# A two-layer attention, memory and expert network on one core: later turns, earlier fetches, and the memory's gradient on another engine

## The chip, the cores and the metric

The kernel runs on one core of a Trainium2 chip. The metric is the device time of one execution in microseconds (us). The engines are named as in the profile: PE is TensorE (matmuls), PEld its weight loads, DVE is VectorE, ACT is ScalarE, POOL is GpSimd, and SP is SyncE, which here issues nearly all DMA transfers from one in-order queue.

## The reference

The input `x` has 16 sequences of 512 tokens with 128 features, in float32. There are two layers, and each adds two branches to its input:

```python
xn = layernorm(x)
x  = x + memory(xn) + block0(xn)     # layer 0
xn = layernorm(x)
x  = x + attn1(xn) + moe1(xn)        # layer 1
```

`memory` is a small network that is trained while it reads. The sequences are cut into 8 chunks of 64 tokens, and the chunks follow one another; in each, the gradient of a loss is taken over all sequences at once:

```python
def mem_fwd((w0, w1, ln), x):
    h = silu(x @ w0.T); y = h @ w1.T
    return x + rmsnorm(y, ln)
loss  = mean((v_c - mem_fwd(p, k_c))**2 * th_c)
grads = grad(loss)(mem)
clip  = min(1 / (sqrt(sum(sum(g*g) for g in grads)) + 1e-6), 1)
surp  = eta_c * surp - grads * clip
mem   = beta_c * mem + surp
...
return mem_fwd(mem_f, q)             # read-out of all tokens with the final memory
```

`block0` is a convolution over tokens, attention with 16 heads of 8 features, a layernorm, and 8 experts of width 512 that all see every token and are weighted by a softmax gate. `attn1` is causal attention with 16 heads; its context goes through a convolution, and the result is used as the queries of a second causal attention over the same keys and values. `moe1` sends each token to 8 of 32 small experts.

## The kernel before

The kernel is written as Python generators, its stages. A loop, `Turns.run`, goes round all live stages in turns and lets each do one step per turn, up to its next `yield`. PE executes in the order in which the steps were written (`ORDERED`); the other engines' instructions are placed by a scheduler, which keeps those of the later stages of a turn behind the newest maximum (`issue_after`). So the number of turns, and what PE does in each, are fixed when the program is built. `idle(n)` lets n turns pass, `after(...)` waits until a named mark is set, with `lag=n` for n turns more, and `fill` puts in a matmul without use where a turn has too little work for PE.

**Attention.** The backbone of nearly every turn is one group of scores in each of two passes. `largest` computes scores (`s<-kx,qx`) into a PSUM buffer of which there is one (`p1=1`), and DVE takes their maxima `nm` (L387 for causal groups of 512 or 384 columns, which add the mask and reduce in one instruction; L396 otherwise). With causal attention the groups of 256 and 128 columns are packed two or four heads to a buffer; their diagonal blocks get the mask by an add, one for each of the two row groups `r` (L395), before L396. The maxima are transposed, go out to `top`, and come back as two more rows of the queries `qx` (L413 to L417). Some turns later, set by `lag` in `back`, `weighted` computes the scores the other way round (`s<-qx,kx`, also with one buffer), ACT takes the exponential `e`, POOL cuts it to the causal triangle (L471), and PE multiplies with the values (`pc`).

**Experts of layer 0.** `ffn(b)` handles one sequence: it loads the accumulator `ac` and the transposed tokens `x1T`, fetches the weights `ew1` and `ew2` of expert 0, idles 2 turns, and then runs 64 units, `first(i)` (hidden layer, `phe` and ACT's `hTe`) and `second(i)` (back to the features, `pye`). A credit of `TURN` ns per turn, less the other PE work of the turn, says how many units run. Each weight is fetched one expert ahead. `x1T` has one buffer, the weights two each.

**Memory.** `scan` runs the 8 chunks one after the other beside the attention of layer 0. `step(c)` turns the keys, computes the hidden layer (`hidden`), and then the gradient in two halves of four token tiles: `gradient(0)` from turn 7 of the step, `gradient(1)` from turn 11. With `yh` the normalised output and `kv` keys minus values, DVE computes `gq = yh*ln*ln + kv*ln` in one half's buffer; POOL had made `kv*ln` (L878) and `ln*ln` (L813). `m` is the row mean of `gq*yh`, and `gq + yh*m`, scaled by ACT, is the gradient that goes back. The gradient of the norm's weight `ln` is made apart from it: `norm_gradient`, from turn 16, lets POOL compute `gy = (yh*ln + kv)*yh*th` over all eight tiles in four passes of 128x1024 (L904 to L910). It first waits until the projections of chunk c+1 are read, since `gy` shares its buffer with their input `xc`. `project(c)` makes keys and values two chunks ahead.

**Read-outs.** After the last chunk, `readout(b)` starts every 6 turns: it projects the queries, normalises them (POOL, L1000 and L1001), idles 3 turns, transposes them, applies the memory, and copies the result to `yq`, always in the buffer `hT1`; POOL adds the rest and the sum is stored to `acc` (L1035).

**Layer 1.** From turn `t0` on, `middle(b)` starts every 44 turns; `front1(b)` loads the transposed tokens and, after 2 turns, projects them.

## Time and profile before

| | |
|---|---|
| runs, median (lowest to highest) | 3922.72 us (3920.65 to 3936.18), 3 runs |
| the profiled execution, its own time | 3921.06 us |
| its span in the profile | 3919.1 us |
| PE busy, of the span | 3463.3 us (88%) |
| DVE, ACT, POOL busy | 2389.2, 2152.6, 1658.1 us |
| mean granted TensorE clock | 0.960 |
| DMA moved | 370.50 MB, mean 95 GB/s |

The profile is of one execution. Its busy times are sums over the span; a row of the groups gives source line, engine, operation, what is written and read, the count, busy time, mean time of one, and the idle time just before with what ended it. Times inside the span, such as "at 335 us", count from its start. In this execution the last read-out is stored at 1581.5 us, and layer 1's attention fills most of the rest.

### The profile page before, as it was taken

The numbers are of one execution on the slowest core, as the hardware profiler recorded it, in microseconds if no ns is written. First come the engines' busy times: TensorE is split into PE (matmuls) and PEld (weight loads), VectorE is DVE, ScalarE is ACT, GpSimd is POOL, SyncE is SP. The second block draws the span as 40 slices with busy tenths as digits, with TensorE's granted clock in tenths as the row PEclk, the third lists the DMA queues.
The fourth block names the chain that finished last, engine by engine and source line by source line (L and its number), as shares of the span: only waits on it lengthen the run. The fifth ranks groups of instructions, "written<-read, shape, count | busy, mean of one in ns | idle before, by whom it ended". The sixth has DMA issues, their size and how long they took to land. (4 is left out here: it accounts for less than half of the span.)

```text
span 3919.1 us, 62028 instructions
## 1 busy us (share of the span) xinstructions
PE 3463.3 (88%) x22267; PEld 1898.2 (48%) x22267; DVE 2389.2 (61%) x5187; ACT 2152.6 (55%) x3687; POOL 1658.1 (42%) x2562
## 2 busy tenths in 40 slices
PE   5889888889899888999999999999999999987877
PEld 2445444445444444445555555555555555543343
DVE  5666646665665545546466666666666666667762
ACT  1555655665566666555555555555555555543443
POOL 5433542453342544323344344424443344333674
PEclk7999999999999999999999999999999999998998
DMA  5222212221322332433434433443334333433343
GB/s 159 64 64 70 67 51 80 64 67 39 106 69 87 95 86 77 128 87 104 123 94 117 113 112 102 110 122 111 104 107 121 107 113 101 120 97 84 83 91 86
DMA packets 289938, 370.50 MB, mean 95 GB/s; under 512 B 46008, under 2 KB 141408, under 8 KB 289248
## 3 DMA queue, kind: packets, MB, share of 16 engines
q1 hardware_dynamic: 282464, 359.73, 32.1%
q0 software_dynamic: 7168, 6.82, 1.1%
q8 instruction: 176, 2.88, 0.3%
q14 instruction: 130, 1.06, 0.1%
HBM read 236.59 MB, written 133.25 MB: 94 GB/s over the span
## 5 line engine op out<-in xcount | busy, mean ns | idle before, releaser
L467 ACT ACTIVATE e<-s 128x1024 f32<-128x1024 f32 (+1 forms) x1216 | 1190.7, 979 | 702.7 <-PE s L192 637.0
L396 DVE TENSOR_REDUCE nm<-s 128x2 f32<-128x1024 f32 (+1 forms) x704 | 861.2, 1223 | 683.9 <-PE s L192 676.3
L387 DVE CUSTOM_DVE_ANT_0 s<-s,sb_const 128x512 f32<-128x512 f32 (+1 forms) x1024 | 647.6, 632 | 543.1 <-PE s L192 524.3
L471 POOL TENSOR_SCALAR_AFFINE_SELECT e<-e 128x128 f32<-128x128 f32 (+2 forms) x1408 | 467.8, 369 | 1003.2 <-ACT e L467 1000.9
L192 PE MATMUL s<-kx,qx 64*128 64x512 f32 (+3 forms) x3072 | 622.0, 432 | 236.8 <-DVE nm L396 132.1
L192 PEld LDWEIGHTS s<-kx,qx 64*128 64x128 f32 x3072 | 275.2, 188 | 895.6 <-issue 275.3
L192 PE MATMUL pc<-e,vp 128*32 128x512 f32 (+3 forms) x6144 | 642.3, 506 | 26.9 <-POOL e L471 26.5
L585 PEld LDWEIGHTS pye<-ew,hTe 128*128 128x128 f32 x4096 | 514.7, 195 | 141.4 <-issue 126.0
L585 PE MATMUL pye<-ew,hTe 128*128 128x128 f32 x4096 | 581.7, 286 | 0.8 <-DMA ew<-in_ew 0.8
L577 ACT ACTIVATE hTe<-phe,sb_cols 128x512 f32<-128x512 f32 x512 | 353.7, 691 | 404.7 <-PE phe L192 402.8
L192 PE MATMUL phe<-x1T,ew 128*128 128x512 f32 x1024 | 538.4, 610 | 14.1 <-DMA x1T<-x1d 6.7
L192 PE MATMUL s<-qx,kx 64*128 64x512 f32 (+3 forms) x3072 | 511.3, 359 | 34.3 <-ACT e L467 25.7
L593 POOL TENSOR_TENSOR ac<-ac,y 128x512 f32<-128x512 f32 x128 | 164.8, 1288 | 399.7 <-ACT y L592 397.4
L192 PEld LDWEIGHTS s<-qx,kx 64*128 64x128 f32 x3072 | 290.3, 190 | 77.1 <-ACT e L467 54.6
L395 DVE TENSOR_TENSOR s<-s,sb_const 128x256 f32<-128x256 f32 (+1 forms) x384 | 199.9, 521 | 150.8 <-PE s L192 138.4
L192 PEld LDWEIGHTS pc<-e,vp 128*32 128x32 f32 x6144 | 151.9, 110 | 255.8 <-issue 172.9
L192 PEld LDWEIGHTS phe<-x1T,ew 128*128 128x128 f32 x1024 | 160.2, 196 | 32.4 <-issue 8.2
L592 ACT ACTIVATE y<-pye,pr 128x128 f32<-128x128 f32 x512 | 146.6, 369 | 42.7 <-PE pye L585 37.9
L387 DVE DVE_READ_ACCUMULATOR2_ANT nm<- 128x1 f32 x1024 | 144.7, 141 | 0.0
L199 PE MATMUL fill<-sb_pb,sb_const 128*128 128x512 f32 (+2 forms) x238 | 122.5, 603 | 10.8 <-DMA sb_pb<-in_pb 10.4
L205 POOL TENSOR_SCALAR rs_t<-ss 128x4 f32<-128x4 f32 (+1 forms) x56 | 12.0, 215 | 197.4 <-ACT sq L258 195.8
L967 POOL TENSOR_TENSOR cl<-cl,phalf 128x1 f32<-128x1 f32 x8 | 4.5, 568 | 190.1 <-ACT cl L966 190.1
(294 smaller groups left out, 3991.8 us busy)
## 6 DMA issues: line engine op xcount, KB each, us to landing
ew<-in_ew SPq DMA_DIRECT2D x256, 256.0 KB
kx<-rk SPq DMA_DIRECT2D x192, 256.0 KB
qx<-rq SPq DMA_DIRECT2D x128, 256.0 KB
rq<-hi SPq DMA_DIRECT2D x64, 256.0 KB
rq<-lo SPq DMA_DIRECT2D x64, 256.0 KB
rk<-hi SPq DMA_DIRECT2D x64, 256.0 KB
rk<-lo SPq DMA_DIRECT2D x64, 256.0 KB
qx<-r SPq DMA_DIRECT2D x64, 256.0 KB
```

The source lines that it names most:

```text
L192: nc.tensor.matmul(o, lhsT=lhsT, rhs=rhs, start=start, stop=stop)
L199: nc.tensor.matmul(o[:, 0:n], lhsT=ident, rhs=cell[0][:, 0:n], start=True, stop=True)
L205: nc.gpsimd.tensor_scalar(t, src, scale, eps, ALU.mult, ALU.add)
L387: newest[0] = nc.vector.tensor_tensor_reduce(out=sv[:, r, 0, :], in0=sv[:, r, 0, :], in1=row["caus"][:, S - n :], scale=1.0, scalar=-BIG, ...
L395: nc.vector.tensor_tensor(dg, dg, bc(row["caus"][:, S - P :], 1, per), ALU.add)
L396: newest[0] = nc.vector.tensor_reduce(nm[:, qt, :, t : t + per], sv, AX.X, ALU.max)
L467: nc.scalar.activation(e[:, :, 0 : per * n], s[:, :, 0 : per * n], AF.Exp, scale=SCALE)
L471: cleared[0] = nc.gpsimd.affine_select(out=ev[:, r, :, 0:P], in_=ev[:, r, :, 0:P], pattern=[[0, per], [1, P]], compare_op=ALU.is_ge, fill= ...
L577: nc.scalar.activation(hs[i], ph, AF.Relu, bias=col("fb", i))
L585: nc.tensor.matmul(pye[0][:, t, :], lhsT=h[:, t * P : (t + 1) * P], rhs=w2[e][:, f, :], start=(f == 0 and t == 0), stop=(f == 3), skip_gro ...
L592: nc.scalar.mul(y[:, t, :], pye[0][:, t, :], pr[:, t, e : e + 1])
L593: nc.gpsimd.tensor_tensor(ac, ac, y, ALU.add)
```

## The change

1. The causal mask is added to both row groups by one instruction instead of two.
2. `fetch0(b)` loads `x1T` and starts the fetches of expert 0. The last `first` unit of `ffn(b-1)` calls it, if the tokens are ready; otherwise `ffn(b)` does and idles 3 turns.
3. The gradient of the memory and that of the norm's weight are made from shared products: `gy = (yh*ln + kv)*yh` per half on DVE, then `gy*ln` for the row mean, and POOL only multiplies `gy` by `th`. `norm_gradient`, `ln2` and the product `kv*ln` are gone. The second half starts at turn 9, not 11.
4. A read-out idles 5 turns before its transpose, and keeps its result in the buffers of `h` and `ds` by turns.
5. `back` lags 5 turns behind the maxima, not 4; `front1` idles 3 turns, not 2.
6. `t0` is 480; it was the turn in which the scan ended, 482, where that is later.

```diff
-                    for r in range(2):
-                        dg = sv[:, r, :, n - P : n]
-                        nc.vector.tensor_tensor(dg, dg, bc(row["caus"][:, S - P :], 1, per), ALU.add)
+                    dg = sv[:, :, :, n - P : n]
+                    nc.vector.tensor_tensor(dg, dg, bc(bc(row["caus"][:, S - P :], 1, per), 1, 2), ALU.add)
...
+    def fetch1(w1, w2, e):
+        w1[e] = ff.tile([P, DFF], F32, tag="ew1", bufs=2, name="ew1")
+        nc.sync.dma_start(w1[e], a["ew1"][:, e, :])
+
+    def fetch2(w1, w2, e):
+        w2[e] = ff.tile([P, 4, D], F32, tag="ew2", bufs=2, name="ew2")
+        nc.sync.dma_start(w2[e], a["ew2"][:, e])
+
+    def fetch0(b):
+
+        x1T = ff.tile([P, S], F32, tag="x1T", bufs=1, name="x1T")
+        nc.sync.dma_start(x1T, x1d[1, b])
+        fetched[b] = x1T, {}, {}
+        fetch1(*fetched[b][1:], 0)
+        fetch2(*fetched[b][1:], 0)
...
-        x1T = ff.tile([P, S], F32, tag="x1T", bufs=1, name="x1T")
-        nc.sync.dma_start(x1T, x1d[1, b])
-        w1, w2 = {}, {}
...
-        fetch1(0)
-        fetch2(0)
-        yield from idle(2)
+        if b not in fetched:
+            fetch0(b)
+            yield from idle(3)
+        x1T, w1, w2 = fetched.pop(b)
...
             nc.scalar.activation(hs[i], ph, AF.Relu, bias=col("fb", i))
+            if i == n - 1 and ("x1", b + 1) in done:
+                fetch0(b + 1)
...
             def before():
-                nc.gpsimd.tensor_tensor(ln2, ln, ln, ALU.mult)
...
-                nc.gpsimd.tensor_tensor(tq, kv[:, a4, :], bc(ln, 1, 4), ALU.mult)
                 yield from idle(3)
                 nc.vector.tensor_tensor(yq, yq, bc(ry[:, a4], 2, D), ALU.mult)
                 nc.gpsimd.tensor_tensor(tr[:, a4], ry[:, a4], th[:, a4, c], ALU.mult)
                 yield
-                nc.vector.tensor_tensor(gq, yq, bc(ln2, 1, 4), ALU.mult)
-                yield
-                nc.vector.tensor_tensor(gq, gq, tq, ALU.add)
-                yield
-                nc.vector.tensor_tensor(tq, gq, yq, ALU.mult)
-                yield
+                nc.vector.tensor_tensor(gq, yq, bc(ln, 1, 4), ALU.mult)
+                yield
+                nc.vector.tensor_tensor(gq, gq, kv[:, a4, :], ALU.add)
+                yield from after(("read", c + 1) if c + 1 < NC else ("read", c))
+                if q == 0:
+                    late["gy"] = s1.tile([P, NT, D], F32, tag="gy", name="gy")
+                gy = late["gy"][:, a4, :]
+                yield
+                nc.vector.tensor_tensor(gy, gq, yq, ALU.mult)
+                yield
+                nc.vector.tensor_tensor(tq, gy, bc(ln, 1, 4), ALU.mult)
+                yield
+                nc.gpsimd.tensor_tensor(gy, gy, bc(th[:, a4, c], 2, D), ALU.mult)
                 nc.vector.tensor_reduce(m[:, a4], tq, AX.X, ALU.add)
                 nc.vector.tensor_scalar(m[:, a4], m[:, a4], -1.0 / D, None, ALU.mult)
                 yield
+                nc.vector.tensor_tensor(gq, gq, bc(ln, 1, 4), ALU.mult)
+                yield
                 nc.vector.tensor_tensor(tq, yq, bc(m[:, a4], 2, D), ALU.mult)
-                yield
                 nc.vector.tensor_tensor(gq, gq, tq, ALU.add)
+                yield
                 yield
                 for t in range(4):
                     nc.scalar.mul(gq[:, t, :], gq[:, t, :], tr[:, 4 * q + t : 4 * q + t + 1])
-                yield
-
-            def norm_gradient():
-
-                yield from after(("read", c + 1) if c + 1 < NC else ("read", c))
-                gy = late["gy"] = s1.tile([P, NT, D], F32, tag="gy", name="gy")
-                nc.gpsimd.tensor_tensor(gy, yh, bc(ln, 1, NT), ALU.mult)
-                yield
-                nc.gpsimd.tensor_tensor(gy, gy, kv, ALU.add)
-                yield
-                nc.gpsimd.tensor_tensor(gy, gy, yh, ALU.mult)
-                yield
-                nc.gpsimd.tensor_tensor(gy, gy, bc(th[:, :, c], 2, D), ALU.mult)
...
-                (7, gradient(0)), (11, gradient(1)), (16, norm_gradient()),
+                (7, gradient(0)), (9, gradient(1)),
...
             nc.gpsimd.tensor_tensor(q, q, bc(rq, 2, D), ALU.mult)
-            yield from idle(3)
+            yield from idle(5)
...
-            y = s1.tile([P, TB, D], F32, tag="hT1", name="yq")
+            y = s1.tile([P, TB, D], F32, tag=("h", "ds")[b % 2], name="yq")
...
-        yield from after(("tops", layer, b, i, c), lag=4)
+        yield from after(("tops", layer, b, i, c), lag=5)
...
         nc.sync.dma_start(xT, xt[1, b])
-        yield from idle(2)
+        yield from idle(3)
...
-    TBB, t0 = 44, max(turns.turn, 480)
+    TBB, t0 = 44, 480
```

More of the change, by code (lines that the diff above doesn't have):

```diff
@@ L506, in conv @@
         mm(o[:, 0 : S - 1], w(2), src[:, 1:S], start=False)
-    credit = [0.0]
+    credit, fetched = [0.0], {}
+    def fetch1(w1, w2, e):
[10 more added lines that the diff above has]
+        fetch2(*fetched[b][1:], 0)
     def ffn(b):
@@ L515, in ffn @@
         nc.sync.dma_start(flat(ac), x1d[0, b])
-        x1T = ff.tile([P, S], F32, tag="x1T", bufs=1, name="x1T")
-        nc.sync.dma_start(x1T, x1d[1, b])
-        w1, w2 = {}, {}
-        def fetch1(e):
-            w1[e] = ff.tile([P, DFF], F32, tag="ew1", bufs=2, name="ew1")
-            nc.sync.dma_start(w1[e], a["ew1"][:, e, :])
-        def fetch2(e):
-            w2[e] = ff.tile([P, 4, D], F32, tag="ew2", bufs=2, name="ew2")
-            nc.sync.dma_start(w2[e], a["ew2"][:, e])
-        fetch1(0)
-        fetch2(0)
-        yield from idle(2)
+        if b not in fetched:
+            fetch0(b)
+            yield from idle(3)
+        x1T, w1, w2 = fetched.pop(b)
         pr = sm.tile([P, TB, EXP0], F32, tag="pr", bufs=2, name="pr")
@@ L566, in gate @@
             yield
-        hs, pye = {}, [None]
+        hs, pye, n = {}, [None], 4 * EXP0
         def first(i):
@@ L572, in first @@
             if e + 1 < EXP0 and f < 2:
-                (fetch1, fetch2)[f](e + 1)
+                (fetch1, fetch2)[f](w1, w2, e + 1)
             ph = work("phe")
@@ L594, in second @@
                 drop()
-        n = 4 * EXP0
         units = [(first, 0)]
@@ L605, in ffn @@
             credit[0] = min(credit[0] + TURN - load_ns[0], 4000)
-            n = int(max(credit[0] + 500, 0) // 1000)
+            more = int(max(credit[0] + 500, 0) // 1000)
             if pools["pairs"]:
-                n = n // 2 * 2 if "values" not in locks or n > 3 else 0
-            for fn, u in units[at : at + n]:
+                more = more // 2 * 2 if "values" not in locks or more > 3 else 0
+            for fn, u in units[at : at + more]:
                 if held[0] >= pools["work"] - (fn is second and u % 4 == 0):
@@ L809, in step @@
             eb = s1.tile([P, 2 * INTER + D], F32, tag="eb", name="eb")
-            ln2 = sm.tile([P, D], F32, tag="ln2", bufs=2, name="ln2")
             def before():
-                nc.gpsimd.tensor_tensor(ln2, ln, ln, ALU.mult)
                 yield from idle(4)
@@ L891, in gradient @@
                 yield
+                nc.vector.tensor_tensor(gq, gq, bc(ln, 1, 4), ALU.mult)
+                yield
                 nc.vector.tensor_tensor(tq, yq, bc(m[:, a4], 2, D), ALU.mult)
+                nc.vector.tensor_tensor(gq, gq, tq, ALU.add)
                 yield
-                nc.vector.tensor_tensor(gq, gq, tq, ALU.add)
                 yield
```

## The prediction

> **What bounds the kernel now.** I read the page first (busy shares and granted clock), then the waits of TensorE over the whole span, then the costly groups with their shapes kept apart, and last the timeline of one bad stretch.
>
> ```profile
> PE 3463.3 (88%) x22267; PEld 1898.2 (48%) x22267; DVE 2389.2 (61%) x5187; ACT 2152.6 (55%) x3687; POOL 1658.1 (42%) x2562
> ...
> PEclk7999999999999999999999999999999999998998
> ```
>
> TensorE (PE) is busy for 88% of 3919.1 us at a nearly full clock. Its instructions stand in the order that the planner wrote. The change takes no matmul out and puts none in, apart from fillers: laid out, the program has 1,275 turns where it had 1,276, and 118 fillers where it had 119. So what can be won lies in the 456 us in which PE stands still (3919.1 less 3463.3), and each part must be costed by the PE waits that it ends. The waits of PE, waiter, releaser, us in total, times, longest:
>
> ```profile
> PE s L192 <- DVE nm L396: 132.1, 145, 5.9
> PE s L192 <- DVE nm L387: 57.5, 101, 1.5
> ...
> PE pjq L192 <- DMA xT<-xt: 11.5, 7, 5.0
> ...
> PE tp L244 <- POOL rq L1001: 9.8, 4, 4.7
> ...
> PE s L192 <- DMA qx<-top: 7.8, 5, 2.7
> PE phe L192 <- DMA x1T<-x1d: 6.7, 1, 6.7
> ...
> PE pgt L192 <- DMA x1T<-x1d: 4.3, 2, 3.5
> ...
> PE tp L244 <- ACT yq L1028: 4.3, 1, 4.3
> PE ppq L192 <- ACT yq L1028: 4.2, 1, 4.2
> ```
>
> The reader should see two kinds: many short waits for VectorE's (DVE) maxima, because the first score pass owns one PSUM buffer and the next scores must wait until `nm` is read, and a few long waits for transfers or for the read-outs. The groups by form (busy us, mean ns):
>
> ```profile
> L395 DVE TENSOR_TENSOR s<-s,sb_const 128x256 f32<-128x256 f32 x256 | 110.4, 431 | 110.6 <-PE s L192 105.2
> L395 DVE TENSOR_TENSOR s<-s,sb_const 128x512 f32<-128x512 f32 x128 | 89.5, 699 | 40.3 <-PE s L192 33.2
> ...
> L883 DVE TENSOR_TENSOR gt<-yh,ln 128x512 f32<-128x512 f32 x16 | 28.7, 1794 | 0.0
> L885 DVE TENSOR_TENSOR gt<-gt 128x512 f32<-128x512 f32 x16 | 25.2, 1578 | 0.0
> ```
>
> The last two rows are the surprise: the same shape takes 0.68 us at its shortest (L883: 0.679 to 2.841). The timeline from 325 to 345 us shows why, POOL (GpSimd) first, then DVE, then PE:
>
> ```profile
> 326.72 2.36 POOL L904 TENSOR_TENSOR gy<-yh,sb_rowsA 128x1024 f32<-128x1024 f32 x1 [4.21 <-DVE m L890]
> 329.16 2.69 POOL L906 TENSOR_TENSOR gy<-gy,v 128x1024 f32<-128x1024 f32 x1
> ```
> ```profile
> 327.77 1.87 DVE L892 TENSOR_TENSOR gt<-yh,m 128x512 f32<-128x512 f32 x1
> 329.56 2.84 DVE L883 TENSOR_TENSOR gt<-yh,ln 128x512 f32<-128x512 f32 x1
> ```
> ```profile
> 334.25 0.79 PE L192 MATMUL s<-kx,qx 64*128 64x512 f32 x2 [2.21 <-DVE nm L396]
> ```
>
> While POOL works on the norm's gradient (L904 to L910), each DVE product with two SBUF inputs lasts until about half a microsecond after POOL's own instruction ends. The maximum queued behind it is late, PE stands for 2.2 us, and its next matmuls run slow (the eight `pye` at 335.4 take 2.07 us, 1.16 us ten us earlier).
>
> **Part 1, the memory's gradient.** Per chunk POOL loses two L878 products, three of four L904 to L908 passes and L813: 21.3 + 19.9 + 21.5 + 21.5 + 3.6 = 88 us over 8 chunks. It keeps the product with `th`, in two halves (17.3 us). DVE gains two 128x512 products per half, 32 x 0.68 = 22 us. What it may lose is the excess of L880 to L894 over their shortest times: (865-675)+(1794-679)+(1578-675)+(832-627)+(1158-653)+(992-658) = 3,252 ns, times 16 = 52 us; the instructions that overlap L904 to L910 carry 40 us of it, those that overlap other POOL work 10. Some 8 us will remain or return under the `th` halves (about 1.1 us each, 16 of them) and some 15 under the products of the next chunk's keys. DVE thus comes out about even or 15 us lower, but without its lumps.
>
> On the path: the eight stretches with L904 to L910 (197-211, 323-338, 457-471, 591-606, 731-746, 867-885, 1003-1020, 1127-1141) last 122 us, PE is busy for 88.5, so idle for 33.5. PE's idle share from 200 to 1200 us is 11.5%, which would be 14 us; the excess is 20. The granted clock in the eight averages 0.91 against 0.97 around them, another 5 us of slower matmuls. I take -20 of these 25. The new wait for the next chunk's projections (`read`, c+1) now stands inside each half, before the buffer `gy` is taken; DVE's later steps of that half are behind it, then `back` and `pgr`. Laid out, `pdh` still follows the first `py` by 17 turns in the first chunk and the last chunk's `pn` moves from turn 370 to 368, so it costs nothing; its cover is that the projections end some ten turns into the step.
>
> [...] The trace has 30 such products that overlap no POOL work and show no excess, and POOL loses 88 us at this place, so I keep -20; the other end is the slower rival below.
>
> **Part 2, one masked add for both row groups.** 256 instructions of 431 ns become 128 of 699, 128 of 699 become 64 of about 1,235 (699 plus twice 268, the step from 256 to 512 elements): 163 ns saved each time, 192 x 0.163 = 31 us of DVE. PE's waits for L396 after 1600 us, where only these shapes exist, are 36.1 us in 60 waits up to 3560 and 13.3 in 13 behind it: at most 73 x 0.163 = 12 us. I take -8. [...] the pair of row groups runs together (two 64x512 in 0.50 us), so a first half has almost nothing to start on early.
>
> **Part 3, turns for transfers.** (a) `front1` waits one turn more, about 2.9 us: of 11.5 us seven waits, the longest (5.0) keeps 2: -9. (b) `back` lags 5 turns: the 7.8 us for the rows of maxima, none over 2.7: -7. (c) `fetch0` sends `x1T` and expert 0's weights at the last first unit of the previous block instead of behind the load of `ac`, which on SP's queue waits for the previous block's store: 6.7 + 4.3 + 0.8 (`ew`) = 11.8, take -10. It also takes two or so turns out of the gap between blocks (the last block's last unit moves from turn 1125 to 1103), which only moves work between turns: 0 (its cover is that PE idles alike in turns with and without expert units, 0.16 to 0.41 us a turn after turn 600). On SP's in-order queue the `x1T` load now waits for PE's last `phe`, and whatever stands behind it waits too; in the new order two expert weights, then a row of zeros and stores follow at the first such place. Bounds: 0, or one turn of PE (2.9 us) in each of 15 blocks, +43; SP already stands in hundreds of such waits (355 us for `pye`) with the transfers covered, so near 0. Sum -26; since a PE wait also lets DVE and POOL catch up, I count -20.
>
> **Part 4, read-outs.** Two more turns (7 us) before the transpose of `rq` cover the four waits of 9.8 us, longest 4.7. The result in the buffers of `h`/`ds` by turns, not always in `hT1`, ends ACT's 15.3 us for the store `acc<-yq`, and with it PE's 4.3 + 4.2 + 1.8 for `yq`. Together 20, take -14: POOL's queue, which is what was late, is next in line. `h` and `ds` come free for read-out b+2 only after the store of b, 12 turns on, so no new wait. The last read-out's product stays in turn 476.
>
> **Sum.** -20 - 8 - 20 - 14 = -62; a quarter goes to waits that take their place, mainly `nm` (PSUM for scores is still single): -46. From the profiled execution's own 3921.06 us (span 3919.1) that gives 3875; the median of the runs shown is 1.7 us above it: **3877 us**, 1.2% less. A measurement of this kernel tells about 0.5%, 20 us, from no change.
>
> **Rivals.**
> *The waits only change their names* (0.15): the 190 us for `nm` stay, and a PE freed from a transfer runs into DVE one turn later. For it: both score passes own one buffer each, DVE is 61 to 67% busy. Against it: the removed waits are mostly longer than 2 us, the `nm` waits mostly under 1. About -6: 3916.
> *The prefetch holds SP's queue* (0.10): parts 1, 2 and 4 come (-42, less a quarter, -31), part 3's gain of 20 is lost, and of its bound of +43 some 5 are not covered: 3921 - 31 + 5 + 2 = 3897.
> *DVE becomes the pace of the scan* (0.13, the slower side): the two halves now run 2 turns apart, not 4, so 8 turns of each chunk, 64 in all, hold two gradient steps beside the 1.22 us maximum. A turn there lasts 3.3 us (208 turns from 292 to 979 us). If the products take 1.58 us, as L885 did, DVE needs 1.22 + 3.16 = 4.4: 1.1 x 64 = +69, against -31 from the other parts: 3960. It cancels those parts from a mean of 1.28 us on and makes the kernel 0.5% slower from 1.43. For it: L883 and L885 are above that today. Against it: their blocker leaves POOL.
>
> **How the numbers follow.** The forecast has 0.62 (its own range 3845 to 3902). Faster by over 0.5%: 0.61 + 0.02 + 0.08 = 0.71; within 0.5%: 0.17; slower: 0.12. Range 3840 to 3930: the forecast's low end and the no-change case are in it, the slow case out.
>
> **What would show it.** Right: DVE's `gt` products near 0.7 us, no PE wait over 2 us beside them, POOL's busy time some 85 us lower; L395 at 192 instructions of 0.70 and 1.24 us; no waits left for `qx<-top`, `x1T`, `yq`. Wrong: `gt` products still above 1.3 us, SP waiting for `phe` with `kx` or `qx` loads late behind it, or PE's waits for `nm` up by what the others fell.

## The result, and the profile after

The changed kernel takes 3905.7 us (median of five runs, 3899.98 to 3908.47) where the kernel before takes 3922.7: a ratio of 0.9944, with a 95% interval of 0.9929 to 0.9959. The medians are 17 us apart; the ratio says 0.56% less, which is 22 us. The direction was forecast; the size was not, since the forecast was 46 us. In the experiments further down, "us against before" is always worked out from the ratio to the kernel before on the same chip, times 3922.7; by that measure the changed kernel stands at -22 us.

The page of the changed kernel, the rows of busy time and of the clock:

```profile
span 3905.3 us, 61944 instructions
...
PE 3452.3 (88%) x22265; PEld 1887.3 (48%) x22265; DVE 2325.2 (60%) x5027; ACT 2156.1 (55%) x3687; POOL 1578.2 (40%) x2522
...
PEclk7999899999999999999999999999999999997999
```

Two subtractions say most of it. DVE is relieved of 64 us (2389.2 to 2325.2) and POOL of 80 (1658.1 to 1578.2), as planned. But the idle time of PE, in which the whole gain was to lie, is 3905.3 - 3452.3 = 453.0 us where it was 455.8. Whatever waits were ended, others of the same size came. The waits of PE over the whole span (waiter, releaser, us in total, times, longest):

```profile
PE s L192 <- DVE nm L395: 145.1, 141, 3.7
PE s L192 <- DVE nm L387: 50.4, 84, 2.0
...
PE s L192 <- issue: 32.6, 20, 2.4
PE s L192 <- DMA kx<-rk: 29.0, 6, 12.9
PE s L192 <- ACT e L466: 26.9, 36, 8.1
...
PE s L192 <- DMA qx<-top: 3.5, 3, 2.0
```

The waits for the transfer of `x1T` are gone, those for `yq` are down to 0.7 us, POOL's for `rq` are gone too (two for DVE's L741 are left, 5.7 and 1.2 us), and `qx<-top` has halved. Three things stand out. L395 (it was L396) has not fallen with the shorter adds: 145.1 us where it was 132.1. `kx<-rk` is at 29.0 us with one wait of 12.9, where before it had 10.1. And the longest wait for ACT's exponential is 8.1 us, where it was 2.2.

The groups of the gradient, by form (busy us, mean ns, idle before):

```profile
L894 DVE TENSOR_TENSOR gy<-gt,yh 128x512 f32<-128x512 f32 x16 | 16.6, 1038 | 0.0
L888 DVE TENSOR_TENSOR gt<-gt,v 128x512 f32<-128x512 f32 x16 | 13.4, 836 | 0.0
...
L904 DVE TENSOR_TENSOR gt<-yh,m 128x512 f32<-128x512 f32 x16 | 10.8, 675 | 0.0
```

The lump is gone: these are the two slowest and the fastest of the gradient's products with two SBUF inputs, and none is above 1.04 us in the mean, where L883 had 1.79 and L885 1.58. The merged add has the two durations that were estimated (699 and 1,235 ns):

```profile
L394 DVE TENSOR_TENSOR s<-s,sb_const 128x512 f32<-128x512 f32 x128 | 89.6, 700 | 146.8 <-PE s L192 146.3
...
L394 DVE TENSOR_TENSOR s<-s,sb_const 128x1024 f32<-128x1024 f32 x64 | 78.9, 1232 | 97.7 <-PE s L192 97.7
```

To see where the time went, I laid the trace over the planned turns: every matmul record belongs to a known turn, and the time from the first matmul of one turn to that of another is a stage. In us, added up from the traces; the columns behind "after" are experiments told below.

| turns | before | after | lag 4 in layer 1 | lag 4 in both | only lag 5 in layer 1 | only the merged add | best version |
|---|---|---|---|---|---|---|---|
| 60-380, the scan | 1043.9 | 1037.0 | 1039.7 | 1028.1 | 1044.1 | 1044.0 | 984.7 |
| 380-486, read-outs | 370.3 | 346.4 | 344.3 | 339.8 | 367.1 | 367.1 | 340.4 |
| 486-520, layer 1 begins | 113.4 | 98.6 | 100.2 | 104.9 | 113.2 | 113.4 | 102.4 |
| 520-1100, layer 1 with experts | 1692.9 | 1735.6 | 1693.2 | 1664.2 | 1760.9 | 1674.8 | 1662.8 |
| 1100-1170 | 187.8 | 192.4 | 190.7 | 186.4 | 195.6 | 181.0 | 185.7 |
| 1170 to the end | 313.7 | 299.1 | 298.1 | 289.6 | 318.9 | 311.0 | 295.4 |

The last row ends with the last matmul. A stage that an edit leaves alone mostly repeats within 0.2 to 3 us between two profiles (the scan before and with only lag 5 in layer 1: 1043.9 and 1044.1; the read-outs: 370.3 and 367.1). The longest one, turns 520 to 1100, is less steady: with the gradient alone (below), which leaves PE's plan there as it was, it took 1703.5 us, 10.6 more than before. So differences of more than some 10 us can be read there. The read-outs gain 24 us and the start of layer 1 gains 15: both in the direction forecast. The scan gains only 7. And layer 1, of which the forecast expected a gain, is 47 us longer in turns 520 to 1170, and 33 us longer from turn 520 to the end. (The two figures differ because the experts' units end at turn 1103 instead of 1125, so turns 520 to 1100 hold 11 units more, and PE's busy time in them is 19 us higher. The columns that are compared below, "after" with "lag 4 in layer 1" and "before" with "only lag 5" or "only the merged add", have the same units in these turns, but for one.) So there are two questions: what is slower in layer 1, and where is the gain of the scan?

The first has a place. This is the timeline of PE, and then of DVE, in one passage of layer 1 in the changed kernel (start, us, instruction, and in brackets the idle time before it):

```profile
2127.30 1.02 PE L192 MATMUL phe<-x1T,ew 128*128 128x512 f32 x2
2128.26 0.51 PE L192 MATMUL s<-kx,qx 64*128 64x256 f32 x4
2128.60 0.39 PE L192 MATMUL s<-qx,kx 64*128 64x512 f32 x2
2128.92 0.64 PE L192 MATMUL pc<-e,vp 128*32 128x128 f32 x16
2130.91 0.50 PE L192 MATMUL s<-kx,qx 64*128 64x256 f32 x4 [1.34 <-DVE nm L395]
```
```profile
2128.80 0.70 DVE L394 TENSOR_TENSOR s<-s,sb_const 128x512 f32<-128x512 f32 x1 [3.13 <-PE s L192]
2129.54 1.22 DVE L395 TENSOR_REDUCE nm<-s 128x4 f32<-128x1024 f32 x1
```

From the first score matmul of the packed group at 2128.26 to the end of its maximum at 2130.76 is a chain of 2.5 us, and the one score buffer is not free until then. PE has only this group's scores, the other scores and 16 short `pc` matmuls to do in that turn, 1.3 us of work and no expert units, so it stands. In the turn before, it did expert units (the last of them is `phe`, at 2127.30).

My theory (A in the expectations) was that `lag=5` brings this about in layer 1: it moves the value products of a group by one turn, the planner's credit then gives the expert units to other turns, and the turns without units fall on the packed groups, whose chain on DVE is the longest. The rivals were that the merged add is to blame, by its one longer instruction, that other parts of the change are, or that it is the clock.

### The profile page after: what moved, and what is told of

It is laid out like the page before. It is cut to its first block, busy times and chain, and to the rows that moved or that the text cites. A ratio compares the mean times of both kernels' runs of the same rounds, so it can differ in the third digit from the quotient of the medians.

```text
span 3905.3 us, 61944 instructions
## 1 busy us (share of the span) xinstructions
PE 3452.3 (88%) x22265; PEld 1887.3 (48%) x22265; DVE 2325.2 (60%) x5027; ACT 2156.1 (55%) x3687; POOL 1578.2 (40%) x2522
## 4 chain that ended last, share of the span: by engine, by line
PE 67%; DVE 15%; POOL 6%; ACT 5%; issue 4%; DMA 3%; SPq 1%; POOLq 0%; ACTq 0%; DVEq 0%
PE s L192 17%; PE pye L591 12%; PE pc L192 11%; PE phe L192 11%; DVE nm L395 6%; DVE s L387 3%; PE tp L244 2%; DVE s L394 2%; PE pgr L192 2%; ACT e L466 2%; PE tpc L244 1%; PE pq L192 1%; PE pcv L192 1%; PE pj L192 1%; ACT sq L258 1%
## 5 line engine op out<-in xcount | busy, mean ns | idle before, releaser
L395 DVE TENSOR_REDUCE nm<-s 128x2 f32<-128x1024 f32 (+1 forms) x704 | 861.4, 1224 | 645.3 <-PE s L192 638.0
L387 DVE CUSTOM_DVE_ANT_0 s<-s,sb_const 128x512 f32<-128x512 f32 (+1 forms) x1024 | 646.7, 632 | 531.2 <-PE s L192 513.5
L192 PE MATMUL s<-kx,qx 64*128 64x512 f32 (+3 forms) x3072 | 623.7, 432 | 274.3 <-DVE nm L395 145.1
L192 PE MATMUL pc<-e,vp 128*32 128x512 f32 (+3 forms) x6144 | 658.9, 518 | 33.4 <-POOL e L470 33.2
L394 DVE TENSOR_TENSOR s<-s,sb_const 128x512 f32<-128x512 f32 (+1 forms) x192 | 168.4, 877 | 244.5 <-PE s L192 244.0
L387 DVE DVE_READ_ACCUMULATOR2_ANT nm<- 128x1 f32 x1024 | 144.5, 141 | 0.0
```

The lines of the kernel that those rows point to most:

```text
L192: nc.tensor.matmul(o, lhsT=lhsT, rhs=rhs, start=start, stop=stop)
L387: newest[0] = nc.vector.tensor_tensor_reduce(out=sv[:, r, 0, :], in0=sv[:, r, 0, :], in1=row["caus"][:, S - n :], scale=1.0, scalar=-BIG, ...
L394: nc.vector.tensor_tensor(dg, dg, bc(bc(row["caus"][:, S - P :], 1, per), 1, 2), ALU.add)
L395: newest[0] = nc.vector.tensor_reduce(nm[:, qt, :, t : t + per], sv, AX.X, ALU.max)
```

## The experiments

### The lag, in layer 1 alone

One line of the changed kernel; layer 0 stays as it is.

```diff
-        yield from after(("tops", layer, b, i, c), lag=5)
+        yield from after(("tops", layer, b, i, c), lag=4 if layer else 5)
```

> The changed kernel with the lag of 4 turns in layer 1 alone (5 stays in layer 0). Theory A (the longer lag moves the light turn, the one with 8 value products and no expert units, onto the turn between two groups of 256 columns, whose chain on VectorE, mask add and maximum, is the longest of a turn): PE's idle time between those two groups falls from 57 us (turns 520 to 1100) to below 20, some 15 come back between the last group of 384 columns and the first of 256, waits for the rows of maxima come back by up to 4 us; about 3875 us, 30 less than the changed kernel's 3905.7. Theory B (the merged mask add makes PE wait, since it can begin only when both row groups are done): the waits stay where they are and the time stays within 8 us of 3905.7. Theory C (the loss in layer 1 is the expert work that now ends 22 turns earlier): also within 8 us.

Measured: 3862.9 us, ratio 0.9836 (0.9812 to 0.9859), 64 us below before and 42 below the changed kernel. Turns 520 to 1100 fall from 1735.6 to 1693.2 us, and all stages ahead of them stay within 3 us. The same passage in this kernel, PE:

```profile
2084.35 0.65 PE L192 MATMUL pc<-e,vp 128*32 128x128 f32 x16
2085.57 0.50 PE L192 MATMUL s<-kx,qx 64*128 64x256 f32 x4 [0.57 <-DVE nm L387]
...
2086.23 0.66 PE L244 MATMUL tpc<-sb_const,cs 128*128 128x128 f32 x4
2086.73 1.06 PE L591 MATMUL pye<-ew,hTe 128*128 128x128 f32 x8
2087.62 1.02 PE L192 MATMUL phe<-x1T,ew 128*128 128x512 f32 x2
2088.57 0.51 PE L192 MATMUL s<-kx,qx 64*128 64x256 f32 x4
```

The light turn with its 16 `pc` now stands one turn earlier, behind a group of 384 columns (L387), whose chain is shorter: 0.57 us of waiting. The turn between the two packed groups holds expert units, and there is no wait at all. The waits of PE from 1600 to 3560 us show the same thing as a sum, first of the kernel before, then after, then of this experiment:

```profile
PE s L192 <- DVE nm L387: 49.9, 82, 1.5
PE s L192 <- DVE nm L396: 36.1, 60, 2.1
```
```profile
PE s L192 <- DVE nm L395: 81.1, 70, 1.8
PE s L192 <- DVE nm L387: 37.7, 57, 1.6
PE s L192 <- issue: 25.6, 15, 2.4
```
```profile
PE s L192 <- DVE nm L387: 66.7, 84, 1.5
PE s L192 <- DVE nm L395: 29.2, 27, 1.9
```

L395 goes from 81.1 back to 29.2 us. Added up from the matmul records of turns 520 to 1100, the idle time of PE ahead of a score group, by the pair of groups (50 pairs of each of the first four kinds, us; "packed" are two heads of 256 columns, "four" four heads of 128):

| previous, next group | before | after | this | after with two adds (below) | only lag 5 (below) |
|---|---|---|---|---|---|
| causal 384, packed | 18.5 | 1.7 | 19.5 | 1.7 | 1.0 |
| packed, packed | 18.8 | 57.4 | 13.3 | 66.5 | 59.5 |
| packed, four | 7.9 | 6.9 | 3.5 | 8.4 | 19.9 |
| four, causal 512 | 21.9 | 37.3 | 15.5 | 43.1 | 33.8 |
| others | 27.9 | 30.6 | 41.4 | 30.0 | 38.6 |

With lag 5 the wait between the two packed groups triples: 57.4 us over 50 turns is 1.15 us each. In the planned order of the changed kernel the turn of the first packed group holds on average 7.7 `pc` products and next to no expert work (0.16 `pye` and 0.04 `phe` products, where a unit has four and one); with lag 4 it holds 0.64 `pc` products, and with them 3.4 `pye`, 0.86 `phe` and 3.5 `tpc`. So the edit moved what theory A says, and the named wait went with it.

### The lag put into the kernel before

```diff
-        yield from after(("tops", layer, b, i, c), lag=4)
+        yield from after(("tops", layer, b, i, c), lag=5 if layer else 4)
```

> The kernel before with the lag of 5 turns in layer 1 alone. Theory A: the idle time between the two groups of 256 columns rises from 19 us to about 65 (with two adds it is some 8 worse than in the changed kernel), the 7.8 us of waits for the rows of maxima fall to about 3; about 3950 us, 25 to 30 more than before. Theories B and C: 3915 us, the 7.8 us less.

Measured: 4005.7 us, ratio 1.0203 (1.0183 to 1.0223), 80 us above before. The sign was expected, the size was not. PE's waits from 1600 to 3560 us:

```profile
PE s L192 <- DVE nm L396: 88.0, 71, 2.6
PE s L192 <- DVE nm L387: 41.6, 40, 1.5
```

Turns 600 to 1000 are 58 us longer than before, of which PE idles 38; the other 20 are slower matmuls. The clock records show it: between 1600 and 3400 us the clock was at half for 143 us, against 65 before, and the mean clock of the execution is 0.951 against 0.960. So the lag costs more in this kernel than the 42 us above. Its two adds make the chain on DVE longer by 0.16 us in each turn in which nothing covers it, but over 50 such turns that is 8 us; the rest of the difference, the slower matmuls among it, is not attributed.

### The merged add, taken out of after and put into before

```diff
-                    dg = sv[:, :, :, n - P : n]
-                    nc.vector.tensor_tensor(dg, dg, bc(bc(row["caus"][:, S - P :], 1, per), 1, 2), ALU.add)
+                    for r in range(2):
+                        dg = sv[:, r, :, n - P : n]
+                        nc.vector.tensor_tensor(dg, dg, bc(row["caus"][:, S - P :], 1, per), ALU.add)
```

> The changed kernel with two mask adds again, one for each row group; everything else, and the order on PE, as in the changed kernel. Theory A: each add pair costs 0.16 us more on the path in the turns that end on VectorE, about 3915 us (10 more). Theory B: the first add starts earlier and PE waits less: about 3885 us.

Measured: 3959.9 us, ratio 1.0078 (1.0057 to 1.0099): 1.0078 / 0.9944 is 53 us above the changed kernel, where I had expected about 10. DVE's own time is only 28.6 us longer (2353.8 against 2325.2). In turns 520 to 1100, 36 us longer, PE idles 16 us more and its matmuls take 20 us more; the time at half clock from 1600 to 3400 us is 133 us against 92. The opposite edit, the merged add alone in the kernel before:

> The kernel before with the merged mask add alone. Theory A, and the 8 us of the prediction: 3912 to 3917 us, PE's waits for the maxima of the packed groups in layer 1 down from 36 us to about 28. Theory B: slower than before, about 3935 us.

Measured: 3894.4 us, ratio 0.9915 (0.9894 to 0.9936), 33 us below before. DVE loses 31.3 us of busy time by it (2389.2 to 2357.9), and the stages that hold these groups, from turn 520 on, are 27.6 us shorter, so nearly the whole of that saving is on the path. PE's waits from 1600 to 3560 us:

```profile
PE s L192 <- DVE nm L387: 50.7, 83, 1.5
PE s L192 <- DVE nm L395: 28.0, 26, 1.9
```

The row of L396 fell from 36.1 to 28.0, by the 8 us that I had forecast, and in that reading the forecast was right. But the time fell by four times as much. Added up from the records, PE's idle time ahead of score groups in turns 520 to 1100 fell by 18.6 us (95.0 to 76.4), and the turns from 1100 to the end are 9 us shorter. The rows that name `nm` don't hold all of PE's idle time ahead of the scores: of the 18.6 us, 10.5 are in waits for `nm` of the packed groups, and 7.0 are in waits that the profile puts down to PE's own `pc` and `tp`. All of the latter stand ahead of the group that follows four heads of 128 columns, where the chain on DVE is add and maximum, too ("four, causal 512" in the table above). So the merged add is no suspect. Of the parts that were tried alone it is the largest gain, and more so with lag 5.

### Is part of it the clock? Fillers in the light turns

In the changed kernel each turn of layer 1 without expert units got a filler (48 of them; PE has 96 more matmul records).

```diff
-        if clock[0] - at_ffn[0] > 2 and n > 0 and held[0] < pools["work"]:
+        if (clock[0] - at_ffn[0] > 2 or light[0]) and n > 0 and held[0] < pools["work"]:
...
+            light[0] = more == 0 and clock[0] > 520
```

> The changed kernel with one filler matmul (about 256 columns, without use) in each turn of layer 1 in which the experts get no unit: 48 fillers more, nearly all in the turn between the two groups of 256 columns, where PE idles 1.15 us. Theory D (what the longer lag costs is half idle time and half the clock that is taken back after the nearly empty turn): the stretches at half clock between 1600 and 3560 us fall from 25 to 15 or fewer, PE's useful matmuls run faster, 3880 to 3895 us although PE has more to do. Theory A without the clock (only the idle time counts): the fillers sit in idle time, 3900 to 3910.

Measured: 3907.7 us, ratio 0.994 (0.9922 to 0.9957): no change. PE's busy time rose by 39 us and its idle time fell by 35, and the time stayed. The time at half clock from 1600 to 3400 us was 92 us, as without the fillers. So the chain on DVE sets the length of these turns, and what PE did in its pauses was neither gain nor loss. That the clock carries half of the lag's cost (D) isn't shown by this; that the filler would raise it was wrong.

### The gradient alone, and the two stalls of the scan

The second question was the scan. The gradient's rewrite alone, put into the kernel before:

> The kernel before with the gradient part alone (shared products, POOL keeps only the product with th, second half at turn 9). Part 1 of the prediction: 20 us less, 3900 to 3905 us, turns 60 to 380 down from 1044 us to 1024. If the stalls at 445 and 682 us are made by this part (theory E), they show here too and the gain is 5 to 10 us: 3912 to 3918 us.

Measured: 3920.7 us, ratio 0.9972 (0.9959 to 0.9984): 11 us less, a little over half of the 20. In the profiled execution turns 60 to 380 are only 4 us shorter than before (1039.5). The trace names what took the rest. The timelines of the changed kernel around 440 us, SP's issues, then POOL, then PE:

```profile
439.66 0.33 SPq L516 DMA_DIRECT2D ew<-in_ew  x1
453.89 0.32 SPq L1116 DMA_DIRECT2D x1d<-x  x1
454.39 0.32 SPq L364 DMA_DIRECT2D kx<-rk  x1
```
```profile
443.56 2.69 POOL L806 TENSOR_TENSOR v<-k,v 128x1024 f32<-128x1024 f32 x1
...
448.05 3.14 POOL L229 TENSOR_SCALAR x<-x,ln_mv,ln_rs 128x128 f32<-128x128 f32 x4
...
452.61 1.26 POOL L237 TENSOR_TENSOR x<-x,sb_rows 128x512 f32<-128x512 f32 x1
```
```profile
457.55 0.76 PE L192 MATMUL s<-kx,qx 64*128 64x512 f32 x1 [12.93 <-DMA kx<-rk]
```

POOL works through the keys of the next chunk (to L806) and only then normalises a sequence for the experts (L229 to L237, ending at 453.87). The store of that result, L1116, is the next entry of SP's in-order queue and waits for it for 14 us. Behind it in the queue stands the load of `kx`, which has nothing to do with either, and PE stands for 12.93 us until `kx` lands. The experiment with the gradient alone has the same stall; in the kernel before, PE has no wait for `kx` at all from 200 to 1200 us. With the gradient alone, in that window:

```profile
PE s L192 <- DMA kx<-rk: 14.3, 2, 12.5
PE s L192 <- ACT e L467: 13.8, 20, 2.2
```

The second stall of the changed kernel is at ACT:

```profile
691.17 0.60 ACT L848 ACTIVATE sg<-pp 128x512 f32<-128x512 f32 x1 [9.02 <-POOL ds L854]
```

A sigmoid waits for a buffer (`sg`, two of them) that POOL reads late, behind the same two jobs. ACT's later work stands behind the sigmoid, exponentials among it, and the next score matmul waits 8.1 us. But this stall is not the gradient's alone: with the gradient alone the longest wait for `e` is 2.2 us (the second row above), and in the changed kernel with lag 4 in both layers (below) it is 2.2 us in that window, too. With lag 4 in layer 1 only it is 8.1 us. So it depends on the lag of 5 in layer 0. My theory for the scan (E) had taken both stalls for the gradient's: it gives its 20 us, and the two take them back. Two mends test it, made on the kernel with lag 4 in layer 1. First the store is issued from POOL's own queue, where it stands behind the normalisation whose result it stores:

```diff
-        nc.sync.dma_start(x1d[0, b], flat(x1))
+        nc.gpsimd.dma_start(x1d[0, b], flat(x1))
```

> The changed kernel with lag 4 in layer 1 (the first experiment's), and the store of x1 after its layernorm issued from POOL's queue instead of SP's. Theory E (the gradient's gain was taken back by two new stalls, one of them this store, which on SP waits for POOL and holds the loads of kx behind it): the stall of 12.9 us at 445 us goes, 3848 to 3853 us. Theory F (POOL's late layernorm itself holds PE, the queue is only where it shows): the stall comes back under another name, within 4 us of 3863.

Measured: 3847.5 us, ratio 0.9794 (0.9765 to 0.9823), 16 us less than without it. Turns 100 to 200 took 325.0 us where they took 335.8; the waits for `kx` fell from 27.1 us (longest 13.2) to 14.5 (longest 8.9). Second, `sg` gets a third buffer as well:

```diff
-                sg = s1.tile([P, 2, INTER], F32, tag="sg", bufs=2, name="sg")
+                sg = s1.tile([P, 2, INTER], F32, tag="sg", bufs=3, name="sg")
```

> As the one before, and three buffers for the sigmoids of the hidden layer (sg) instead of two. Theory E: ACT no longer waits 9 us at 682 us for a buffer that POOL's backlog holds, so the exponentials behind it are on time; the 8.1 us stall goes too: 3838 to 3846 us. Theory F: no change against the one before.

Measured: 3828.2 us, ratio 0.9747 (0.972 to 0.9774), another 18 us less, more than expected. But the stall that the buffer was to end is still there:

```profile
670.07 0.60 ACT L848 ACTIVATE sg<-pp 128x512 f32<-128x512 f32 x1 [7.22 <-POOL ds L854]
```

PE waits 7.2 us behind it, where it waited 9.0 without the third buffer. So the edit pays, and not by the reason given. The two profiled executions are 33 us apart, of which turns 60 to 380 make 25 and turns 200 to 300 alone 14 (331.7 to 317.4). Only 5 us of that are in the row of PE's waits for `e` (25.1 to 20.5); the mean clock rose from 0.959 to 0.968, and PE's busy time fell by 25 us. The clock's share is seen, its cause was not tested.

The rival was that these mends help any kernel and have nothing to do with the gradient. So the kernel before got both (and one buffer of `ln2` less, to make room):

> The kernel before (its own gradient, two mask adds, lag 4) with the two mends alone: the store of x1 on POOL's queue and three buffers for sg (ln2 gets one buffer instead of two for the room). Theory E (the gradient's gain was masked by collisions that it moved, and with them gone it is worth its 15 to 20 us): turns 60 to 380 take about 1022 us here, where the kernel with gradient and mends took 1005 and the kernel before 1044; about 3905 us. Theory G (the mends bring all of it, the gradient part next to nothing): about 1005 to 1010 us in those turns, 3890 us.

Measured: 3901.2 us, ratio 0.9923 (0.9909 to 0.9937). The mends are worth 30 us there too. In turns 60 to 380 this kernel takes 1028.8 us, against 1005.1 for the mended one with the new gradient: 24 us less, where the same comparison without mends gives 1043.9 - 1039.7 = 4. So both hold in part. POOL's late work stalls the kernel before as well, in smaller pieces (ACT's longest wait for `sg` in it is 4.1 us), and with the mends the gradient brings what was forecast of it. The kernel with the new gradient also has lag 5 in layer 0 here. The two kernels further down that have lag 4 in both layers take this out: 1043.9 - 1028.1 = 16 us without the mends, 1028.8 - 984.7 = 44 with them. The early fetches are in these figures as well; alone they gave 3 us in these turns.

### The fetches alone

`fetch0` and what calls it, put into the kernel before; nothing else.

> The kernel before with the experts' inputs fetched ahead alone. Part 3c of the prediction: 10 us less, no waits of PE for x1T; about 3918 us. Rival (the fetch holds SP's queue behind PE's last hidden layer): no gain or up to 10 us more, with new waits for kx or qx.

Measured: 3918.8 us, ratio 0.9969 (0.9953 to 0.9984), 12 us less. The waits for the transfer of `x1T` are gone. But the sum hides two opposite parts. In the profiled execution, whose span is that of the kernel before (3919.2 us), turns 60 to 520 are 26 us shorter, and those from 520 to the end are 28 us longer. In the plan the experts' units end at turn 1107 instead of 1125, and layer 1 starts two turns earlier. PE's waits from 1600 to 3560 us, where the kernel before had 49.9 and 36.1 us:

```profile
PE s L192 <- DVE nm L387: 55.0, 70, 1.5
PE s L192 <- DVE nm L396: 54.5, 73, 2.1
```

So the fetches end their waits, and in the plan that they bring about others of nearly the same size stand in layer 1. There are also three new waits for `kx` (2.8, 2.1 and 3.3 us); whether SP's queue makes them was not followed up.

### The read-outs alone

```diff
-            yield from idle(3)
+            yield from idle(5)
...
-            y = s1.tile([P, TB, D], F32, tag="hT1", name="yq")
+            y = s1.tile([P, TB, D], F32, tag=("h", "ds")[b % 2], name="yq")
...
-    TBB, t0 = 44, max(turns.turn, 480)
+    TBB, t0 = 44, 480
```

> The kernel before with the read-outs alone (5 idle turns, results in the buffers of h and ds), and the start of layer 1 at turn 480, since the scan now ends at turn 488. Part 4 of the prediction: 14 to 24 us less, the turns 380 to 486 down from 370 us to about 347; about 3905 us. Rival: part of what those turns lost in the changed kernel is the clock or the gradient's doing, then 360 us and 3917.

Measured: 3960.1 us, ratio 1.0076 (1.0059 to 1.0094): 30 us slower. In its own turns it did what was forecast: 20 us less from 380 to 486, and 12 less from 486 to 520. But layer 1, which it does not touch, takes 77 us longer (turns 520 to 1170). PE's waits from 1600 to 3560 us:

```profile
PE s L192 <- DVE nm L387: 78.6, 91, 1.5
PE s L192 <- DVE nm L396: 40.8, 63, 2.1
PE pjq L192 <- DMA xT<-xt: 29.9, 13, 4.8
```

The loads of `xT` are late 13 times instead of 6, and `nm` costs more as well; the time at half clock rises to 171 us. With the read-outs shifted against a fixed `t0`, layer 1 starts two turns earlier than before and the experts' later units run up to 8 turns later, and `front1` has no third idle turn here. So a part that gains in its own place can lose elsewhere by a mere shift, and parts of this change depend on one another. PE's idle time ahead of `pjq` makes 21 us of the 77 (27.4 against 6.5); how the rest divides isn't settled.

### Without the lag altogether, and how much a mere shift is worth

The changed kernel with `lag=4` in both layers, no mends:

> The changed kernel with the lag of 4 turns in both layers, no mends: the change without its longer lag. If the lag in layer 0 costs by itself, 45 to 60 us less than with lag 4 in layer 1 alone (3863), so 3805 to 3815 us. If the 56 us of the experiment before came from where the collisions and the expert units happened to fall: anywhere from 3830 to 3875, with the scan's two stalls (12.9 and 8.1 us) in other places or gone, since the lag in layer 0 moves them.

Measured: 3818.4 us, ratio 0.9725 (0.9701 to 0.9749). Its page, one row:

```profile
PE 3428.8 (90%) x22257; PEld 1882.5 (49%) x22257; DVE 2340.8 (61%) x5027; ACT 2151.3 (56%) x3687; POOL 1570.6 (41%) x2522
```

In a span of 3812.0 us PE idles for 383 us, 70 less than in the changed kernel. By the ratios, the lag of 5 costs 86 us: 42 in layer 1, and 44 that came when layer 0 got lag 4 too, just under the 45 to 60 of the first expectation. Of this second part, by the stages, some 16 us lie in turns 60 to 486, where the stall of 8.1 us at `sg` is gone and the one at `kx` is still there (13.9 us). Some 42 lie behind turn 520, where the lag is the same in both kernels and only the places of the expert units differ (the single profiles differ by 49 us in all, and turns 486 to 520 lose 5). That made me ask what a shift alone can do: the experts of sequence 4 begin two turns later, in two of the kernels above, the mended one and the best one below.

```diff
         yield from after(("x1", b))
+        if b == 4:
+            yield from idle(2)
```

> The kernel with both mends and lag 5 in layer 0 (3828 us), and the experts of sequence 4 begin two turns later, so that from there on the expert units fall two turns later in layer 1's pattern; no other edit. If the alignment of the units decides: layer 1 (turns 600 to 1170) moves by 10 to 30 us either way. If it doesn't: within 6 us of 3828.

Measured: ratio 0.9718 (0.9696 to 0.974), 11 us less than without the edit, with intervals that overlap. The plan says why this can't be read: the planner's credit made the delay good within two sequences. Of the 1,274 turns only 40, from 507 to 611, have other PE work than without the edit, and most of the difference of the profiles lies behind them, where the plans are alike.

> The fastest version (mends, lag 4 in both layers, 3772 us) with the same shift of two turns. If its 25 us in layer 1 were luck of alignment, they are lost: about 3785 to 3800. If the lag of 4 in both layers earns them: within 6 us of 3772.

Measured: ratio 0.9645 (0.962 to 0.9669), 18 us more. Here the shift stays: from sequence 4 on the units run 2.5 to 6 turns later. So a shift that changes no work and no dependency is worth 18 us, and the read-outs alone, where layer 1 starts two turns earlier, lost 77 us there, 21 of them at `xT`. By its size alone the 42 us of the lag in layer 1 could thus be luck of alignment. What speaks against it is that the time moved the way of the theory both times, with the lag put into one kernel and taken out of the other, and that the wait that theory A names grew and shrank with it (18.8 to 59.5 us, 57.4 to 13.3). The 44 us of the rest are not cleanly attributed: how much of them is such luck is open.

### The best version

The changed kernel with `lag=4` in both layers, the store on POOL's queue and three `sg` buffers.

> The fastest version so far (changed kernel, lag 4 in layer 1, store on POOL, three sg buffers: 3828 us) with lag 4 in layer 0 too. Theory A: in layer 0 all score groups are alike (1024 columns, one maximum), so the turn with the value products meets the same chain wherever it lies: within 6 us of 3828. Rival: the longer lag in layer 0 paid by itself (rows of maxima late), then 3840 or more, with waits of PE for qx<-top before 1600 us.

Measured: 3772.5 us, ratio 0.96 (0.9581 to 0.9619), 157 us or 4.0% below before, and the fastest of all runs.

In its span of 3770.8 us PE is busy for 3414.4 and so idles for 356 us, 97 less than in the changed kernel. I had expected layer 0's lag to matter by under 6 us; it was 58, by the ratios to the mended kernel with lag 4 in layer 1 alone. With the same reserve as above, lag 4 was better in each of the four comparisons.

## Why the prediction was right in direction and wrong in size

**Which step failed.** It was step (b) of part 3, "`back` lags 5 turns: the 7.8 us for the rows of maxima, none over 2.7: -7". The wait was there and it was ended (7.8 to 3.5 us). But the step costed the added turn only by the wait that it ends. It did not ask which turn the value products go to, what leaves that turn because of it, and how long DVE's chain is in it. Measured: +42 us in layer 1, and up to 86 in all. The text came near it on the fetches, with idle time "alike in turns with and without expert units"; as a mean over all turns that was so (0.27 and 0.30 us a turn from turn 600 to 1270), but not for the packed groups, where 18.8 us became 57.4.

**Part 1, -20.** The rows came as forecast: products near 0.7 us (the excess over 675 ns of the seven rows L886 to L905 adds up to some 13 us where 23 were to remain), POOL 80 us lower where 85 were forecast. The size was -11 alone, because the sum did not ask which of POOL's other work would then be late. It was POOL's normalisation behind the next keys, and through SP's queue the loads behind its store. With the store on POOL's queue and the third `sg` buffer, the scan is 24 us shorter than in the kernel before with the same two edits where layer 0 has lag 5, and 44 where it has lag 4, the early fetches included.

**Part 2, -8.** The durations were exact, and the term was too small by a factor of four: -33. The 163 ns were counted for the 73 waits that the profile lists under L396, though the score buffer is single in all 192 groups, and behind the groups of four heads the profile puts waits of the same kind down to PE's own `pc` and `tp`. The upper end was in the text, 31 us of DVE, and was not carried into the range. Two adds instead of one cost 33 us in the kernel before and 53 in the changed one.

**Part 3 (a) and (c), -19.** The waits ended: those for `xT` fell from 11.5 to 0.8 us, those for `x1T` are gone, and turns 486 to 520, which held the longest of both (5.0 and 6.7 us), are 15 us shorter. (a) was not tried alone. (c) alone gave 12 us. But the prediction put at 0 what (c) does to the places of the expert units, and with the fetches alone layer 1 was 28 us longer.

**Part 4, -14.** Right in its own turns and too low there (-24 in turns 380 to 486 of the changed kernel). Alone it loses, by what it shifts.

**The sum.** Without step (b), the raw terms come to about -57 us (the lag's 7 count as 5 after the discount from 26 to 20); without the lag, the kernel gains 108 (ratio 0.9725). Of the difference, the merged add gives 25 and the read-outs 10 or more; some 16 us are not attributed and may be luck of the places. So too little gain was forecast for what works and one cost was overlooked, and the two cancelled in good part. The direction owes something to luck: without the merged add the changed kernel is 0.78% slower than the kernel before, and with only the 8 us forecast for that part it would not have been faster. A quarter taken off for waits that take the place of others was the right thought without the right place.

**The rivals.** That the waits only change their names gives 3916 us and looks close to the 3905.7, and the `nm` rows do stay (189.6 to 195.5 us). But its mechanism falls for the change as a whole: without the longer lag the other edits take 73 us of idle time from PE (455.8 to 383), and the `nm` rows are at 154.5 us. For the fetches alone it holds in part (`nm` 189.6 to 201.7 us). That the prefetch holds SP's queue is not borne out by the fetches alone (-12 us, and new waits for `kx` of 8 us in all); SP's queue was held indeed, but by a store, for 14 us. That DVE becomes the pace of the scan fell: its products are at 0.68 to 1.04 us, and the point of decision was 1.28.

## What to carry to other kernels

A delay that is moved by one turn is to be costed in the order that the planner makes of it: which turn becomes light, and how long the longest chain of the other engines is in just that turn; and before a difference of 10 or 20 us is credited to an edit, a shift without meaning should be tried for comparison and the plan read, whether it did shift. Time saved on an engine that alternates with another over a single buffer can count in nearly every round, here 27.6 of 31.3 us, and not only where the profile lists a wait under that engine's name. On SP's queue the store that waited 14 us for POOL held up the load of `kx` behind it, and PE stood for 12.93 us; such a store belongs into a queue that has nothing urgent behind it, and here that was one line for 16 us.

## What the runs showed of the hardware that I had not expected

Two pauses of PE of nearly the same length were followed by matmuls of different speed. After 1.34 us of waiting at 2130.91 in the timeline above, the four score matmuls took 0.50 us. In the kernel before, after 1.32 us:

```profile
2256.84 0.51 PE L192 MATMUL s<-kx,qx 64*128 64x256 f32 x4 [0.57 <-DVE nm L387]
...
2259.69 0.80 PE L192 MATMUL s<-kx,qx 64*128 64x256 f32 x4 [1.32 <-DVE nm L396]
2260.26 0.66 PE L192 MATMUL s<-qx,kx 64*128 64x512 f32 x2
```

The same four matmuls took 0.80 us, and the next ones 0.66 where two of the same form just ahead took 0.40 and 0.49 (at 2255.30 and 2257.24). Summed up, the time at half clock between 1600 and 3400 us was 41 us in the best version, 65 before, 92 after and 171 in the trial of the read-outs. In the trial of the lag on the kernel before, 20 us of slower matmuls stood beside 38 us of waits. With fillers in the changed kernel's light turns the time at half clock was 92 us, as without them.

In the kernel before, the granted clock was 1.00 from 2252.5 to 2259.23 us, 0.86 us into the pause of 1.32 us, and 0.50 from there to 2266.06. In the changed kernel it was 1.00 from 2126 to 2136 us, all around the pause of 1.34 us. So the length of the pause alone does not tell the two cases apart; what does was not shown.
